# Rows of an attention layer's residual: turned by TensorE before, by 32x32 blocks on VectorE and by DMA after

## The chip, the core and the metric

One core of a Trainium2 chip runs the whole program. TensorE (PE) multiplies matrices, VectorE (DVE), ScalarE (ACT) and GpSimd (POOL) do the elementwise work, SyncE (SP) and, for small things, ACT and POOL issue DMAs. The metric is device time of one execution in microseconds; before the change it is 2252.64 us, the median of 3 runs (2251.83 to 2252.95). All data are float32.

## What is computed

The input x is 16 batches of 1024 nodes with 256 features, with one adjacency matrix for all. Each batch goes through two residual layers; the first holds a small network with two attentions (one over all nodes, one masked), the second one masked attention. Cut to what matters:

```python
# layer 0
h = maximum(layernorm(x), 0)
out = relu(h @ mlp1_w + b1); residual = out                # 256 -> 512
out = elu(gat(out, None, W_fc, a_fc, slope=0.2))           # over all 1024 nodes
out = relu((elu(out) + residual) @ mlp2_w + b2)            # 512 -> 256, "o" below
res2 = out
out = elu(gat(out, adj, W_hand, a_hand, slope=0.2)) + res2 # masked
x = x + relu(out)
# layer 1
h = maximum(layernorm(x), 0)
x = x + relu(masked_softmax_attention(h @ W, a, adj, slope=0.01))
# gat(v): g = v @ W; e[i,j] = leaky_relu(f1[i] + f2[j]); softmax over j; sum_j att[i,j] g[j]; elu
```

The order of the nodes is free wherever it is summed over (index j), as long as the mask's rows and the vectors of a sum follow the same order.

## The kernel before

**Tiling.** 1024 nodes are 8 tiles of 128, in two halves of 4 tiles (`NH` = 2, `TH` = 4). A matrix product contracts over the partitions, so layers that contract over features need features on the partitions ("turned", names that end in T), while the attention's sum and the residual of a batch need nodes on the partitions ("natural"). Turning is done in two ways. `Norm.turn` (L529) and `Dense.natural` (L1030) use transposes of 128x128 on TensorE into PSUM, from which ACT copies them out. `BlockNorm` (L553, first norm of batches 3 to 15) uses VectorE's transpose, which turns each 32x32 block in its place (L572), and then 16 DMAs a half from SP (L582, `move`), which put the blocks where they belong; in those each contiguous run has 32 floats, 128 bytes.

**Stages of a batch.** First norm, `mlp1` (L748), projection for the dense attention (`h`, L762), dense attention through sorting: ranks on DVE (L808 to L815), a scatter of rows by POOL into DRAM (L822), a read of the sorted rows (L866), running sums on DVE (L896, L909) written as tables (L901), gathers from these by POOL (L934: eight "fine", then eight "coarse" that add onto them), the mean (L956, L959), `merge` (L1006 to L1017) back into `resT`. Then `mlp2` (L1024) gives `oT`, two chunks of features by 1024 nodes. `oT` is used twice: as the stationary operand of the projection `pa` (L614) of the first masked attention, and, turned to natural rows, as its residual `o_nat`. `natural` makes `o_nat` for batch b in 4 steps of 4 transposes and one eviction (L1038, L1040), which also subtracts 1. The masked attention makes weights on DVE (L667, `att`, a ring of 8 buffers of 128x256), multiplies (L677) and finishes: two rectified copies (L692, L693), two exponentials (L698, L699), two adds on POOL (L705 with `o_nat`, L706), and DVE's `update` (L710) into x. Second norm, its projection `pb`, a second masked attention (`ob`), and the store.

**Order.** The batches overlap. Nothing is scheduled by the compiler: each step has a nominal time, given by `at` (L471) relative to the batch's base (one base every 142 units), plus a shift from the table `SHIFT` for its place in the list; the steps are sorted by time, and each engine's instructions, those of PE, DVE, ACT and SP, stand in that order. POOL's are held in the same order by dependencies. So an engine that waits for one instruction holds back all behind it. The table has parts: "start", "first" (batch 0), "mid" (1 to 12), "end" (13 to 15). For the mid batches, times relative to the batch's own base:

- `masked_first8`: the 4 steps of `natural` at 4.5, 26.0, 18.2 and 30.2;
- `second_mlp2`: the projections of `oT`, -16.7 to -8.5;
- `masked_first6`: x loaded again at 10; `start51`: the xn of a later batch loaded at 38.7;
- `first_norm7`, `first_norm8`: the moves of the first norm, in the period before;
- `masked_first4`/`masked_first3`: the row of weights, written to DRAM by ACT (`send`) and read back on all partitions by SP (L652).

What a move issues, and the way `o_nat` is made:

```python
for q in range(P // Q):                                     # L580
    nc.sync.dma_start(dst[q * Q:(q + 1) * Q, :, a, :],
                      src[a * Q:(a + 1) * Q, :, q, :])
...
nc.tensor.transpose(ps[:, u * F + c * P:u * F + (c + 1) * P],   # L1038
                    self.oT[:, c, t * P:(t + 1) * P], ident)
...
nc.scalar.activation(self.o_nat[:, 2 * q:2 * q + 2, :],         # L1040
                     ps.rearrange("p (u f) -> p u f", u=2), AF.Identity, bias=neg1)
```

## Time and profile before

| What | Value |
|---|---|
| Median of 3 runs | 2252.64 us |
| Profiled execution, own time | 2251.37 us |
| Its span, first to last instruction | 2249.6 us |
| Granted TensorE clock, mean | 0.998 |
| One steady period (base to base) | 134.2 us |
| DVE, ACT, POOL busy in it | 99 to 101, 77 to 78, 60 to 62 us |
| DMA share and rate in it | 0.65, 169 to 175 GB/s |
| DMA packets in all | 263,870; 124,352 under 512 B |
| Moves of the first norm (hT<-xn) | 416 DMAs of 32 KB |
| First adds of `o_nat` in POOL (L705) | x118, 904 ns |

A line of a group reads: line, engine, operation, output<-inputs, shapes, count, then busy time and mean of one, then the idle time of the engine just before such instructions, and what ended it. In a timeline a line is a run of like instructions: start, length, engine, line, what, count, and in brackets the idle time before it with the one that ended it. In a table of stages the columns are the stage, its length, the busy time of PE, PEld (weight loads), DVE, ACT and POOL with their counts, the granted clock, the share of the DMA engines and GB/s. A busy PE is counted to the modelled end of each matmul; consecutive matmuls overlap.

### The profile page before, as it was taken

How to read it: one execution, taken by the hardware profiler on the slowest of the kernel's cores; microseconds unless marked ns; L12 is line 12 of the kernel's file. 1: busy time of each engine (PE TensorE's matmuls, PEld its weight loads, DVE VectorE, ACT ScalarE, POOL GpSimd, SP SyncE). 2: the span in 40 equal slices, each digit the busy share in tenths (PEclk: the TensorE clock that was granted, in tenths of full speed). 3: DMA queues.
4: the chain of work that ended last, by engine and by line, in shares of the span. 5: the costliest groups of instructions: out<-in, count | busy, mean ns of one | idle time of the engine just before them, and what ended most of it. 6: DMA issues, size and time to landing. Idle time of an engine off the chain costs nothing.

```text
span 2249.6 us, 31025 instructions
## 1 busy us (share of the span) xinstructions
PE 2207.2 (98%) x9754; PEld 1723.4 (77%) x9754; DVE 1643.1 (73%) x4535; ACT 1259.6 (56%) x2797; POOL 954.4 (42%) x1212
## 2 busy tenths in 40 slices
PE   7999999999999999999999999999999999999997
PEld 5767777787877878787787877878787787877776
DVE  7677676777867678776776867677786776858765
ACT  5355745547365564756557375564746557365542
POOL 1163425263452536425263452636435263543620
PEclk9999999999999999999999999999999999999999
DMA  5568466675766757566685666757566585645700
GB/s 197 159 175 196 114 208 154 186 183 148 197 123 200 187 168 190 137 196 148 192 191 147 189 127 194 188 177 189 130 205 144 185 197 153 164 125 169 178 22 28
DMA packets 263870, 368.95 MB, mean 164 GB/s; under 512 B 124352, under 2 KB 175880, under 8 KB 259600
## 3 DMA queue, kind: packets, MB, share of 16 engines
q1 hardware_dynamic: 217088, 202.72, 31.9%
q0 software_dynamic: 45952, 163.99, 28.9%
q8 instruction: 80, 1.31, 0.3%
q14 instruction: 94, 0.77, 0.1%
q10 hardware_dynamic: 656, 0.17, 0.0%
HBM read 226.88 MB, written 126.29 MB: 157 GB/s over the span
## 4 chain that ended last, share of the span: by engine, by line
PE 75%; DVE 6%; DMA 2%; POOL 2%; ACT 1%; issue 1%; POOLq 0%; DVEq 0%; ACTq 0%; SPq 0%
PE oa L677 17%; PE h L762 16%; PE ob L677 14%; PE m L1024 8%; PE m L748 6%; PE pa L614 4%; PE pb L614 3%; PE hpT L1006 2%; DMA got<-coarse,k 2%; DVE attb L667 1%; PE carry L918 1%; PE on L1038 1%; PE nt L536 1%; DVE stats L516 1%; DVE hp L959 1%
## 5 line engine op out<-in xcount | busy, mean ns | idle before, releaser
L677 PE MATMUL ob<-hmb,attb 128*128 128x257 f32 x2048 | 463.9, 380 | 2.2 <-DVE attb L667 1.9
L762 PE MATMUL h<-wfc_sb,resT 128*128 128x257 f32 x2048 | 462.8, 379 | 0.0
L677 PE MATMUL oa<-hma,atta 128*128 128x258 f32 x2048 | 459.9, 382 | 1.8 <-DVE atta L667 1.5
L677 PEld LDWEIGHTS ob<-hmb,attb 128*128 128x128 f32 x2048 | 383.9, 190 | 67.2 <-issue 12.3
L677 PEld LDWEIGHTS oa<-hma,atta 128*128 128x128 f32 x2048 | 384.8, 190 | 59.3 <-DVE atta L667 2.9
L762 PEld LDWEIGHTS h<-wfc_sb,resT 128*128 128x128 f32 x2048 | 380.1, 189 | 59.1 <-issue 7.4
L705 POOL TENSOR_TENSOR posa<-posa,onat 128x256 f32<-128x256 f32 x118 | 106.7, 904 | 546.1 <-ACT posa L693 487.6
L667 DVE SCALAR_TENSOR_TENSOR attb<-rowsb,qwdb,edge 128x256 f32<-128x256 f32 (+1 forms) x536 | 292.1, 563 | 34.6 <-PE ob L677 28.6
L667 DVE SCALAR_TENSOR_TENSOR atta<-rowsa,qwda,edge 128x256 f32<-128x256 f32 (+1 forms) x520 | 257.3, 524 | 51.4 <-DMA rowsa<-row_a 35.6
L934 POOL DMA_INDIRECT got<-coarse,k x124 | 203.4, 1640 | 90.9 <-DMA got<-fine,k 56.6
L748 PE MATMUL m<-hT,w_sb 128*128 128x512 f32 x512 | 236.6, 596 | 1.9 <-ACT rb L719 1.1
L1024 PE MATMUL m<-resT,w_sb 128*128 128x512 f32 x512 | 228.3, 593 | 1.0 <-POOL resT L1017 1.0
L719 ACT ACTIVATE rb<-ob,recb 128x256 f32<-128x256 f32 x128 | 58.5, 474 | 274.9 <-DVE recb L717 248.9
L1017 POOL TENSOR_TENSOR resT<-resT,e 128x512 f32<-128x512 f32 x128 | 165.5, 1295 | 104.9 <-DVE e L1016 96.7
L692 ACT ACTIVATE ea<-oa,reca 128x256 f32<-128x256 f32 x128 | 60.3, 471 | 248.1 <-DVE reca L689 228.7
L934 POOL DMA_INDIRECT got<-fine,k x124 | 126.7, 1022 | 128.5 <-DVE hpd L999 41.9
L1024 PEld LDWEIGHTS m<-resT,w_sb 128*128 128x128 f32 x512 | 94.5, 190 | 102.4 <-issue 93.5
L748 PEld LDWEIGHTS m<-hT,w_sb 128*128 128x128 f32 x512 | 94.2, 191 | 89.0 <-issue 74.7
L822 POOL DMA_INDIRECT sorted<-hnat,place x128 | 128.6, 1004 | 53.9 <-DVE place L815 33.0
L764 ACT COPY hnat<-h 128x257 f32<-128x257 f32 x256 | 90.8, 367 | 104.1 <-PE h L762 101.6
L845 ACT ACTIVATE junk<-r,fs 128x1024 int8<-128x1024 f32 x124 | 142.6, 1150 | 0.9 <-POOL fs L766 0.6
L1016 DVE SCALAR_TENSOR_TENSOR e<-hpT,e 128x512 f32<-128x512 f32 x128 | 87.9, 688 | 53.2 <-ACT e L1010 53.0
(195 smaller groups left out, 3391.2 us busy)
## 6 DMA issues: line engine op xcount, KB each, us to landing
xs<-sorted SPq DMA_DIRECT2D x32, 1028.0 KB
fine<-tt SPq DMA_DIRECT2D x32, 1026.0 KB
fine<-xs SPq DMA_DIRECT2D x32, 1026.0 KB
x<-in_x_dram SPq DMA_DIRECT2D x16, 1024.0 KB
xn<-in_x_dram SPq DMA_DIRECT2D x15, 1024.0 KB
out_dram<-x SPq DMA_DIRECT2D x28, 512.0 KB
hT<-xn SPq DMA_DIRECT2D x416, 32.0 KB
coarse<-carry SPq DMA_DIRECT2D x32, 256.5 KB
```

The source lines that it names most:

```text
L614: nc.tensor.matmul(ps[:, :2 + F], lhsT=hT[:, c, t * P:(t + 1) * P], rhs=self.w_sb[:, c, 0, :], start=(c == 0), stop=(c == FC - 1))
L667: nc.vector.scalar_tensor_tensor(a_t[:, :n * P], self.rows[:, i], self.qwd[:, 1, j:j + 1], edge[:, j, i], op0=OP.max, op1=OP.mult)
L677: nc.tensor.matmul(self.out[t][:, :F + self.ONES], lhsT=self.att[t0, j][:, (t - t0) * P:(t - t0 + 1) * P], rhs=self.hm[:, j, 2:2 + F + sel ...
L705: adder.tensor_add(pos, pos, o_nat[:, t, :])
L748: nc.tensor.matmul(ps, lhsT=w1_sb[:, kc, c * P:(c + 1) * P], rhs=piece(kc, h), start=(kc == 0), stop=(kc == FC - 1))
L762: nc.tensor.matmul(ps[:, :F + 1], lhsT=self.resT[:, kc, t * P:(t + 1) * P], rhs=wfc_sb[:, kc, g, :], start=(kc == 0), stop=(kc == HC - 1))
L764: nc.scalar.copy(self.h_nat[:, t, g, :], ps[:, :F + 1])
L822: made = nc.gpsimd.indirect_dma_start(out=sorted_d[self.b % 2], out_offset=bass.IndirectOffsetOnAxis(ap=self.place[:, t:t + 1], axis=0), i ...
L845: nc.scalar.activation(junk, self.r2, AF.Sign, bias=self.fs[:, 0, t:t + 1], accum_out=self.signs[:, t:t + 1])
L934: nc.gpsimd.indirect_dma_start(out=got[u // n][:, u % n, :], out_offset=None, in_=(coarse_d if coarse else fine_d)[self.b % 2][:, :], in_o ...
L1017: nc.gpsimd.tensor_add(dst, dst, e)
L1024: nc.tensor.matmul(ps, lhsT=w2_sb[:, kc, c * P:(c + 1) * P], rhs=self.resT[:, kc, h * HALF:(h + 1) * HALF], start=(kc == 0), stop=(kc == H ...
```

## The change

`o_nat` of batches 1 to 13 is no longer made by TensorE. DVE turns `oT` in place by 32x32 blocks, a half at a time (`Dense.blocks`), and eight `move` steps of four DMAs each bring the blocks to the partitions of their nodes. So that the DMAs have runs of 1 KB, the features and nodes of a half are laid out anew (`by_rows`): a turned half is a row of four parts of 256 floats, part a holding the nodes whose place in their tile is 32a to 32a+31, from all four tiles. A tile of a turned tensor (`sources`) is then not 128 consecutive nodes but one such part: nodes are permuted within a half wherever they are summed over. `mlp2`, both norms and `mlp1` write and read through that view; the mask's columns are permuted when it is built, and the rows of weights are put back in natural order on their way (`send_row`, `row`). The first norm's moves take the same form, with runs of 1 KB in place of 128 bytes. Batches 0, 14 and 15 still turn on TensorE; since a tile of theirs is now not contiguous, ACT copies each 128x128 piece first. The subtraction of 1 goes from `natural` into the two `update`s. Nearly all entries of `SHIFT` are new (cut below to the ones that the text speaks of).

```diff
-    "mid masked_first8": (0, 19.91, 10.5, 20.85,),
+    "mid masked_first8a": (-7.062,),
+    "mid masked_first8b": (0, 12.185, 12.037, 0, -3.284, 0, 12.142, 11.934,),
-    "mid second_mlp2": (-9.69, -9.64, -7.39, -8.59, -7.35, -8.45, -11.04, -8.66,),
+    "mid second_mlp2": (-13.877, -13.654, -13.893, -15.403, -15.718, -17.262, -17.592, -18.455,),
-    "mid start51": (4.72,),
+    "mid start51": (-41.029,),
...
-        nc.vector.tensor_scalar(valid, valid, wrong[:, 1, t:t + 1], None, op0=OP.max)
+        by_tile = work.tile([P, N], BF16, tag="hp", name=f"by_tile_{t}", bufs=TH)
+        for h in range(NH):
+            lo = h * HALF
+            nc.vector.tensor_scalar(
+                by_tile[:, lo:lo + HALF].rearrange("p (a u i) -> p u a i", u=TH, i=Q),
+                valid[:, lo:lo + HALF].rearrange("p (u a i) -> p u a i", u=TH, i=Q),
+                wrong[:, 1, t:t + 1], None, op0=OP.max)
...
-            nc.tensor.transpose(pt[:, j, :], valid[:, j * P:(j + 1) * P], ident16)
+            nc.tensor.transpose(pt[:, j, :], by_tile[:, j * P:(j + 1) * P], ident16)
...
-    def send_row(dst, col, name):
+    def send_row(dst, col, name, by_tile=False):
...
-        nc.scalar.dma_start(dst.rearrange("o (u i) -> (o u) i", i=P), line)
+        if by_tile:
+            for h in range(NH):
+                nc.scalar.dma_start(
+                    dst[:, h * HALF:(h + 1) * HALF].rearrange("o (u a i) -> (o a) u i", u=TH, i=Q),
+                    line[half(h)].rearrange("a (u i) -> a u i", u=TH))
+        else:
+            nc.scalar.dma_start(dst.rearrange("o (u i) -> (o u) i", i=P), line)
     class Norm:
...
         def turn(self, t):
...
-                self.hT = big.tile([P, FC, N], F32, tag=self.tag, name=f"hT{self.name}", bufs=1)
+                self.hT = big.tile([P, NH, FC * HALF], F32, tag=self.tag, name=f"hT{self.name}",
+                                   bufs=1)
...
-                    nc.scalar.activation(self.hT[:, c, h * HALF:(h + 1) * HALF], self.ps[c],
+                    nc.scalar.activation(by_rows(self.hT[:, h])[:, c],
+                                         self.ps[c].rearrange("p (u a i) -> p u a i", u=TH, i=Q),
...
         def piece(self, c, h):
-            return self.hT[:, c, h * HALF:(h + 1) * HALF]
+            return by_rows(self.hT[:, h])[:, c]
+        def part(self, c, t):
+            return sources(self.hT, c, t)
         def stats_steps(self, h):
...
+        def turned(self, h):
+            return self.get_x()[:, half(h)].rearrange("p t f -> p (t f)")
         def blocks(self, t):
...
-            dst = self.get_x()[:, half(h)].rearrange("p t f -> p (t f)")
-            dst = dst.rearrange("p (c u n) -> p c u n", c=FC, u=TH)
-            nc.vector.transpose(dst[:, :, u, :], self.hn[t])
+            dst = self.turned(h).rearrange("p (q c u i) -> p u c q i", q=P // Q, c=FC, u=TH)
+            nc.vector.transpose(dst[:, u], self.hn[t].rearrange("p (c q i) -> p c q i", c=FC, i=Q))
         def move(self, h, a):
...
-                self.hT = big.tile([P, NH, FC * HALF], F32, tag="hT0", name=f"hT{self.name}",
+                self.hT = big.tile([P, NH, FC * HALF], F32, tag=self.tag, name=f"hT{self.name}",
...
-            src = self.get_x()[:, half(h)].rearrange("p t f -> p (t f)")
-            src = src.rearrange("p (v q i) -> p v q i", q=P // Q, i=Q)
-            dst = self.hT[:, h].rearrange("p (v a i) -> p v a i", a=P // Q, i=Q)
-            for q in range(P // Q):
-                nc.sync.dma_start(dst[q * Q:(q + 1) * Q, :, a, :],
-                                  src[a * Q:(a + 1) * Q, :, q, :])
-        def piece(self, c, h):
-            return self.hT[:, h, c * HALF:(c + 1) * HALF]
+            move_blocks(self.hT[:, h], self.turned(h), a)
+    def move_blocks(dst, src, a):
+        run = FC * HALF // (P // Q)
+        for q in range(P // Q):
+            nc.sync.dma_start(dst[q * Q:(q + 1) * Q, a * run:(a + 1) * run],
+                              src[a * Q:(a + 1) * Q, q * run:(q + 1) * run])
+    def sources(wide, c, t):
+        h, a = divmod(t, TH)
+        lo = (a * FC + c) * P
+        return wide[:, h, lo:lo + P]
+    def by_rows(t):
+        return t.rearrange("p (a c u i) -> p c u a i", a=P // Q, c=FC, i=Q)
     def half(h):
...
-        def __init__(self, get_hT, w_sb, slope, b, which):
-            self.get_hT, self.w_sb, self.slope, self.name = get_hT, w_sb, slope, f"{which}_{b}"
+        def __init__(self, get_part, w_sb, slope, b, which):
+            self.get_part, self.w_sb, self.slope, self.name = get_part, w_sb, slope, f"{which}_{b}"
...
-            hT = self.get_hT()
+            part = self.get_part()
...
-                nc.tensor.matmul(ps[:, :2 + F], lhsT=hT[:, c, t * P:(t + 1) * P],
+                nc.tensor.matmul(ps[:, :2 + F], lhsT=part(c, t),
...
         def send(self):
-            send_row(row_d[self.which][self.b % 2], self.qwd[:, 0, :], f"line{self.name}")
+            send_row(row_d[self.which][self.b % 2], self.qwd[:, 0, :], f"line{self.name}", True)
         def row(self, sent=False):
...
-                for i in (slice(0, PAIR), slice(PAIR, N)):
-                    nc.scalar.copy(self.rows[:, i], rows_ps[:, i])
+                for h in range(NH):
+                    i = slice(h * HALF, (h + 1) * HALF)
+                    nc.scalar.copy(self.rows[:, i].rearrange("p (u a i) -> p a u i", u=TH, i=Q),
+                                   rows_ps[:, i].rearrange("p (a u i) -> p a u i", u=TH, i=Q))
...
         def add(self, t, o_nat, adder):
...
-            adder.tensor_add(pos, pos, o_nat[:, t, :])
+            wide = pos.rearrange("p (c a i) -> p c a i", c=FC, i=Q)
+            adder.tensor_add(wide, wide, o_nat(t))
...
         def update(self, t, xt):
-            nc.vector.scalar_tensor_tensor(xt[:, t, :], self.out[t], 0.0, xt[:, t, :], op0=OP.max,
+            nc.vector.scalar_tensor_tensor(xt[:, t, :], self.out[t], 1.0, xt[:, t, :], op0=OP.max,
...
     class Gnn1(Masked):
...
         def update(self, t, xt):
-            nc.vector.tensor_add(xt[:, t, :], xt[:, t, :], self.out[t])
+            nc.vector.scalar_tensor_tensor(xt[:, t, :], xt[:, t, :], -1.0, self.out[t], op0=OP.add,
+                                           op1=OP.add)
...
         def mlp2(self, h, c):
...
-                self.oT = big.tile([P, FC, N], F32, tag="hT", name=f"oT_{self.b}", bufs=1)
+                self.oT = big.tile([P, NH, FC * HALF], F32, tag="hT", name=f"oT_{self.b}", bufs=1)
...
-            nc.scalar.activation(self.oT[:, c, h * HALF:(h + 1) * HALF], ps, AF.Relu,
+            nc.scalar.activation(by_rows(self.oT[:, h])[:, c],
+                                 ps.rearrange("p (u a i) -> p u a i", u=TH, i=Q), AF.Relu,
...
+        def part(self, c, t):
+            return sources(self.oT, c, t)
+        def blocks(self, h):
+            nc.vector.transpose(self.oT[:, h], self.oT[:, h])
+        def move(self, h, a):
+            if self.o_nat is None:
+                self.o_nat = big.tile([P, NH, FC * HALF], F32, tag="onat", name=f"onat_{self.b}",
+                                      bufs=1)
+            move_blocks(self.o_nat[:, h], self.oT[:, h], a)
+        def natural_rows(self, t):
+            return (self.o_nat[:, t // TH].rearrange("p (a c u i) -> p u c a i", a=P // Q, c=FC,
+                                                     i=Q)[:, t % TH])
         def natural(self, q):
...
-                self.o_nat = big.tile([P, NT, F], F32, tag="onat", name=f"onat_{self.b}", bufs=1)
+                self.o_nat = big.tile([P, NH, FC * HALF], F32, tag="onat", name=f"onat_{self.b}",
+                                      bufs=1)
...
+            h, u0 = divmod(2 * q, TH)
...
-                    t = 2 * q + u
-                    nc.tensor.transpose(ps[:, u * F + c * P:u * F + (c + 1) * P],
-                                        self.oT[:, c, t * P:(t + 1) * P], ident)
-            nc.scalar.activation(self.o_nat[:, 2 * q:2 * q + 2, :],
-                                 ps.rearrange("p (u f) -> p u f", u=2), AF.Identity, bias=neg1)
+                    nodes = by_rows(self.oT[:, h])[:, c, u0 + u]
+                    line = work.tile([P, P], F32, tag="part", name=f"line_{self.b}_{q}_{u}_{c}")
+                    nc.scalar.copy(line.rearrange("p (a i) -> p a i", i=Q), nodes)
+                    nc.tensor.transpose(ps[:, u * F + c * P:u * F + (c + 1) * P], line, ident)
+            for u in range(2):
+                nc.scalar.copy(self.natural_rows(2 * q + u),
+                               ps[:, u * F:(u + 1) * F].rearrange("p (c a i) -> p c a i", c=FC,
+                                                                  i=Q))
...
-        gnn0[b] = Gnn0(lambda b=b: dense[b].oT, wh_sb, SLOPE_A, b, "a")
-        gnn1[b] = Gnn1(lambda b=b: norm2[b].hT, wl_sb, SLOPE_B, b, "b")
+        gnn0[b] = Gnn0(lambda b=b: dense[b].part, wh_sb, SLOPE_A, b, "a")
+        gnn1[b] = Gnn1(lambda b=b: norm2[b].part, wl_sb, SLOPE_B, b, "b")
...
-            at("masked_first8", t0 + 4.5, t0 + 11, each(dense[b].natural, range(NT // 2)))
+            if b == 0:
+                at("masked_first8", t0 + 4.5, t0 + 11, each(dense[b].natural, range(NT // 2)))
+            else:
+                d = dense[b]
+                at("masked_first8a", t0 + 0.5, t0 + 2, each(d.blocks, range(NH)))
+                at("masked_first8b", t0 + 3, t0 + 13, each(d.move, range(NH), range(P // Q)))
...
-            at("masked_first11", end + 1.2, end + 1.2, [lambda t=t: m.combine(t, dense[b].o_nat)])
+            at("masked_first11", end + 1.2, end + 1.2, [lambda t=t: m.combine(t, dense[b].natural_rows)])
...
-                at("masked_first12", end + 2.6, end + 2.6, [lambda t=t: m.add(t, dense[b].o_nat, nc.vector)])
+                at("masked_first12", end + 2.6, end + 2.6, [lambda t=t: m.add(t, dense[b].natural_rows, nc.vector)])
```

## The prediction, made before the result was seen

> **What bounds the kernel now.** I read the busy times first, then the groups by line with shapes kept apart, then one steady period in order of time, then the same period cut into stages.
>
> ```profile
> PE 2207.2 (98%) x9754; PEld 1723.4 (77%) x9754; DVE 1643.1 (73%) x4535; ACT 1259.6 (56%) x2797; POOL 954.4 (42%) x1212
> ...
> L748 PE MATMUL m<-hT,w_sb 128*128 128x512 f32 x512 | 236.6, 596 | 1.9 <-ACT rb L719 1.1 <-ACT hT L540 0.6 <-issue 0.2
> ...
> L1038 PE MATMUL on<-ident,oT 128*128 128x128 f32 x256 | 38.0, 273 | 0.1
> ```
>
> TensorE works in 2207.2 of 2249.6 us. Of the 42.4 us without it, 11.1 lie before its first matmul (it waits for POOL's rstd) and about 10 behind its last product; half of the rest lies in the last batches (93% busy from 2100 to 2200 us). In the steady periods, 134.2 us each, it is busy for all 134.2. So the price of an edit in the middle is what it adds to or takes from TensorE, as long as nothing makes it wait. The busy column is not that price: matmuls overlap, and 273 ns is one latency. The pace stands in the timeline of TensorE, where a row merges a run:
>
> ```profile
> 1110.69 0.60 PE L1038 MATMUL on<-ident,oT 128*128 128x128 f32 x4
> 1111.13 7.13 PE L677 MATMUL oa<-hma,atta 128*128 128x258 f32 x32
> 1118.09 0.60 PE L1038 MATMUL on<-ident,oT 128*128 128x128 f32 x4
> 1118.53 4.52 PE L677 MATMUL oa<-hma,atta 128*128 128x258 f32 x20
> 1122.88 0.60 PE L1038 MATMUL on<-ident,oT 128*128 128x128 f32 x4
> 1123.32 11.56 PE L677 MATMUL oa<-hma,atta 128*128 128x258 f32 x52
> ```
>
> From the start of four transposes to the next product are 0.44 us: 109 ns each. Whether entering such a group costs more is open: runs of products take 0.2177 us each here ((7.13 - 0.38)/31, 0.38 being one latency), by which 32 end just where the next transposes begin; elsewhere they take 0.2143 (14.73 us for 68), by which 0.1 us would be lost: 0 to 0.07 us a group.
>
> **What goes.** Batches 1 to 13 lose `natural`: 13 x 16 = 208 transposes on TensorE and 13 x 4 = 52 evictions on ACT. TensorE: 208 x 0.109 = 22.7 us, and 52 entries at 0 to 0.07, 0 to 3.6; I take 1.3, together **-24 us** (1.8 per period). ACT: 52 x 0.68 = 35 us, not on the path. [...] the rows say 109 ns, as they run back to back, and that TensorE has no free time while DVE has 27%. I go by the rows.
>
> **What is added for it.** Per batch two DVE block transposes of 128x1024 and eight moves of four DMAs (32 KB each). The nearest DVE row:
>
> ```profile
> L572 DVE STREAM_TRANSPOSE xn<-hn 128x256 f32<-128x256 f32 x104 | 42.4, 427 | 0.0
> ```
>
> An estimate from it and the DVE slope between 256 and 512 elements (429 and 688 ns, L710 and L1016, 1.01 ns each): 0.43 + 768 x 0.00101 = 1.2 us, 2.4 us a period. They stand at base -6.6 and +1.2 (nominal times of the table; `on` at base +4.5 ran at 1097.27 us here, that at 18.2 at 1110.69). They wait for the projections that read oT; those stand at base -20, so nothing is held behind them. DVE has gaps there:
>
> ```profile
> 1093.89 0.17 DVE L621 TENSOR_REDUCE exta<-hma 128x1 f32<-128x8 f32 x1 [4.67 <-ACT hma L616]
> ...
> 1105.95 1.28 DVE L667 SCALAR_TENSOR_TENSOR atta<-rowsa,qwda,edge 128x256 f32<-128x256 f32 x3 [4.22 <-DMA rowsa<-row_a]
> ```
>
> Two idle stretches of over 4 us, before the first weights of the masked products: 0 on the end. If that cover is gone, 2.4 us a period of DVE in a stage that has none to spare (below).
>
> The moves on SP: the old ones are the measure.
>
> ```profile
> 1119.11 10.98 SPq L901 DMA_DIRECT2D fine<-xs  x2
> 1130.14 0.50 SPq L335 DMA_DIRECT2D xn<-in_x_dram  x1
> ...
> 1201.31 10.43 SPq L582 DMA_DIRECT2D hT<-xn  x16
> ```
>
> Sixteen issues in 10.43 us, 0.65 each, so 32 new ones take 21 us of SP per period. Half 0's are due at base +3, 16.4, 17.5 and 6.75, half 1's at 4.7, 9.25, 22.6 and 23.7. The first passes ahead of the row's read, while SP idles for it (1092.8 to 1101.3). Two of half 0 queue behind the first table write (issued 1102.2 now), and done by some 1110; two of half 1 queue behind the write of 1119.1, done by some 1127 (8 x 0.65 plus the flight). The first adds that read `o_nat` ran at 1119.05 (tile 0) and about 1134 (tile 4). Margin 7 us or more: 0 on the end. Behind a late move stand the other table writes on SP, and POOL's add, and behind that the gathers.
>
> The first norm's moves become 1-KB runs (416 x 256 packets of 128 B become 416 x 32 of 1 KB). Nothing waits for hT in the steady part (L748's idle is 1.9 us in the run), so 0.
>
> **Layout edits.** mlp1's moving operand becomes 16 runs of 32 floats instead of 512 in a row. No row has such an operand. Below: 0; above: some tenth of its pace (0.43 us, from 1.88 = 3 paces + 0.59), 512 x 0.043 = 22 us. [...] No run here shows it; I take 0. Strided outputs of ACT and DVE: L572's write is already in 32-float runs at 427 ns against 424 for a plain add (L723), so 0. POOL's adds read `o_nat` in 32-float runs: 0 to +0.39 us each (up to the 1295 ns of the 512-wide add, from 904), at most 3.1 us a period on an engine 42% busy; 0, with up to 1.6 us for the four adds between gathers if it bites. The second DMA of `send` costs ACT 0.27 us, 27 times, ahead of time: 0. Masks: 8 DVE writes of 486 ns become 16 shorter strided ones, 0 to 4 us at 20-50 us; I take 1. update's new forms: 429 against 424 ns, 0.
>
> **Batches 0, 14 and 15** keep `natural`, with an ACT copy before each transpose, from a ring of two buffers. A copy is about 0.31 us (414 ns at 256 elements, L698, less 128 x 0.83 ns, slope to L1009's 626). Copies 3 and 4 need transposes 1 and 2 to be over; so TensorE, in order, waits inside each step: 0.27 (transpose) + 0.31 + 0.14 (weight load) - 0.22 + another 0.2 = 0.7 to 0.8 us. Behind the waiting copy stand, on ACT, the scales of hm and the evictions of products, for which TensorE's next banks wait. Twelve steps: **+9 us**; the lower end 0, where TensorE waits anyway (last batch), the upper 20, if ACT's queue is late. I take +7.
>
> **New places.** Two matter. The load of the next xn moves from base +38.7 to base -7.0, in front of the sorted read on SP; the stages show what it leaves:
>
> ```profile
> 1110.00:1120.00 10.00, 10.00 (x51) 8.75 (x51) 10.00 (x25) 3.26 (x8) 0.95 (x1) 1.00 0.47 140
> ...
> 1130.00:1140.00 10.00, 10.00 (x48) 8.74 (x47) 9.83 (x31) 4.00 (x11) 5.34 (x7) 1.00 1.02 220
> ...
> 1160.00:1170.00 10.00, 10.00 (x51) 8.59 (x50) 2.02 (x8) 4.46 (x12) 8.69 (x10) 1.00 1.01 188
> ```
>
> Columns: TensorE, weight loads, DVE, ACT, POOL busy, granted clock (1.00), DMA share, GB/s. DMA is full from 1130 on, when the xn load starts; 1 MB at 220 GB/s is 4.8 us that the gathers get back. It matters, because the gathers end without margin:
>
> ```profile
> 1169.99 0.16 DVE L946 TENSOR_TENSOR den<-got,qd 128x4 f32<-128x4 f32 x1 [6.81 <-DMA got<-coarse,k]
> ...
> 1174.69 0.36 PEld L1006 LDWEIGHTS hpT<-ident,hp 128*128 128x128 f32 x3 [0.29 <-DVE hp L959]
> ```
>
> DVE stands 6.81 us for the gathered rows, and TensorE takes up hp just as it comes. With 1.8 us less TensorE work ahead of it, it would stand here unless the gathers come earlier: 4.8 against 1.8 says that they do. The second: the projections of oT go from base -17...-8 to -20, so the row for the masked weights comes earlier and DVE's 4.22 us shrink, just ahead of the stage where DVE is full (10.00 of 10). I count neither as a gain beyond that, and 0 for the rest of the table.
>
> **Sum.** -24 + 7 + 1 = -16 us. Span 2249.6 becomes 2233.6; this execution took 2251.37, 1.8 more than its span, and the median shown is 1.3 above that. So 2252.6 - 16 = about **2236 us**.
>
> **Rivals.**
> - *The gathers set the period (slower).* Place: hpT at L1006. For: no margin above; xn's load now competes with the sorted read that feeds the same chain. Against: its window was under 80% full. If the chain is as long as before, all 24 us are given back as waits, and the 8 of batches 0, 14, 15 and the masks remain: 2261. It decides from about 1.2 us of new wait per period (16/13). Chance 0.14.
> - *DVE full at 1110-1140.* TensorE reaches the masked products 1.3 us earlier than DVE has weights; for: 10.00 of 10; against: eight weight buffers are 8 x 0.86 = 6.9 us ahead, and the row comes earlier. Half the gain lost: 2252.6 - 12 + 8 = 2249. Chance 0.12.
> - *mlp1's operand is slower.* At the upper bound, +22: 2259; breaks even at 31 ns a matmul (16/512). Chance 0.04.
> - *More falls away*: no waits in batches 0, 14, 15 and 7 us of the scattered ones gone: 2252.6 - 24 + 1 - 7 = 2223. Chance 0.12.
> - The forecast, 2227 to 2245: 0.58.
>
> Measurements of this kernel tell about 0.2% (4.5 us) from no change. Faster: 0.58 + 0.12 + half of DVE's case, 0.76; within: 0.08; slower: 0.16. The range 2219 to 2253 leaves out the two slow cases.
>
> **What would show it.** A steady period of about 132.4 us with TensorE busy throughout; `on` left x48; hpT's wait on hp no longer than now; L946's wait shorter; TensorE idle inside `natural` of batches 0, 14, 15; L748's mean still 596 ns. Wrong, if the period stays at 134 with waits on hp or atta, if POOL waits for the moves of o_nat, or if L748 grows.

## The result, and the profile after

The changed kernel takes 2294.74 us (median of 4 runs, 2288.7 to 2299.17), the kernel before beside it 2252.8 (2251.83 to 2255.87): ratio 1.0183, with 95% interval 1.0171 to 1.0195. The forecast was 2236, range up to 2253; the kernel became 42 us slower. Profiled execution: 2293.65 us, span 2291.9.

The page of the kernel after, its busy times and two groups of its lines (busy us, mean ns | idle before, releasers):

```profile
PE 2213.4 (97%) x9546; PEld 1698.8 (74%) x9546; DVE 1639.5 (72%) x4569; ACT 1253.0 (55%) x2805; POOL 972.4 (42%) x1212
...
L800 PE MATMUL m<-hT,w_sb 128*128 128x512 f32 x512 | 237.9, 599 | 1.5 <-ACT resT L803 1.0 <-ACT hT L576 0.5
...
L1111 PE MATMUL on<-ident,line 128*128 128x128 f32 x48 | 11.9, 318 | 7.2 <-ACT line L1110 4.0 <-DVE qwda L691 3.0
```

The 208 transposes are gone (9754 matmuls became 9546), and mlp1's strided operand costs next to nothing (599 ns for 596). The engine that works most beyond before is POOL, 18 us on an engine 42% busy. So the 42 us are not longer work but waits, and what waits bring with them (last section). To count them I take, for each matmul, the time from its start to the next one's start, less the pace of its size (0.109, 0.217 or 0.429 us for 128, 256 or 512 columns in runs of like matmuls in these traces). Over the whole trace this excess was 35.4 us before and is 104.7 now: 69.3 more, against 22.7 us of transposes saved. The rest, 46.6 us, is what the stretch from the first matmul to the last grew by; what lies ahead of and behind it became 4.3 us shorter, so the span grew by 42.3. Most of it is in the twelve steady periods (third start of `extpsa` to the fifteenth): 7.0 us before, 71.8 now. Where it sits, in TensorE's waits of the kernel after (tile, line, releaser: us in total, times, longest):

```profile
PE oa L727 <- DVE atta L717: 16.9, 29, 1.6
PE extpsb L520 <- DVE extb L670: 15.3, 9, 2.8
PE linea_ps L525 <- ACT qwda L687: 11.6, 13, 0.9
...
PE on L1111 <- ACT line L1110: 4.0, 13, 0.7
```

The same two in the kernel before, where `linea_ps` had no wait:

```profile
PE oa L677 <- DVE atta L667: 1.5, 3, 0.7
PE extpsb L491 <- DVE extb L622: 0.8, 1, 0.8
PE extpsb L491 <- DVE extb L621: 0.8, 1, 0.8
```

A steady period (start of `extpsa` to the next, mean of ten) went from 134.5 to 138.3 us; 132.4 was forecast. TensorE's timeline in one such period, with the idle time and its releaser in brackets:

```profile
1112.83 0.29 PE L520 MATMUL extpsa<-ident,exta 128*128 128x128 f32 x1
1114.01 0.27 PE L525 MATMUL linea_ps<-ident,qwda 128*8 128x128 f32 x1 [0.89 <-ACT qwda L687]
...
1118.42 4.50 PE L727 MATMUL ob<-hmb,attb 128*128 128x257 f32 x20
1123.84 1.98 PE L727 MATMUL oa<-hma,atta 128*128 128x258 f32 x8 [0.92 <-DVE atta L717]
...
1195.70 0.29 PE L520 MATMUL extpsb<-ident,extb 128*128 128x128 f32 x1 [1.16 <-DVE extb L670]
```

`linea_ps` stands directly behind `extpsa`, with no other matmul to cover the short chain between them on DVE and ACT. Before, four matmuls of `mlp1` stood there:

```profile
1095.33 0.27 PE L491 MATMUL extpsa<-ident,exta 128*128 128x128 f32 x1
1095.44 1.88 PE L748 MATMUL m<-hT,w_sb 128*128 128x512 f32 x4
1097.16 0.27 PE L496 MATMUL linea_ps<-ident,qwda 128*8 128x128 f32 x1
```

For the other two waits, DVE's timeline in the same period:

```profile
1123.20 3.65 DVE L717 SCALAR_TENSOR_TENSOR atta<-rowsa,qwda,edge 128x256 f32<-128x256 f32 x9 [5.76 <-DMA rowsa<-row_a]
...
1194.06 1.42 DVE L1011 SCALAR_TENSOR_TENSOR hp<-got,den,part 128x513 f32<-128x513 f32 x2
1195.40 0.16 DVE L669 TENSOR_REDUCE extb<-hmb 128x1 f32<-128x8 f32 x1
```

DVE stood idle 5.76 us for the row, 4.22 before (all 13 such waits: 67.3 us, 35.6 before); TensorE then waits for the weights. And `extb` stands behind two `hp`, 1.42 us together; before, it stood ahead of them:

```profile
1170.68 0.16 DVE L621 TENSOR_REDUCE extb<-hmb 128x1 f32<-128x8 f32 x1
...
1171.64 2.96 DVE L959 SCALAR_TENSOR_TENSOR hp<-got,den,part 128x513 f32<-128x513 f32 x4 [0.72 <-ACT part L956]
```

### The profile page after: what moved, and what is told of

It reads as the page before. It is cut to its first block, busy times and chain, and to the rows that moved or that the text cites. A ratio compares the mean times of both kernels' runs of the same rounds, so it can differ in the third digit from the quotient of the medians.

```text
span 2291.9 us, 31196 instructions
## 1 busy us (share of the span) xinstructions
PE 2213.4 (97%) x9546; PEld 1698.8 (74%) x9546; DVE 1639.5 (72%) x4569; ACT 1253.0 (55%) x2805; POOL 972.4 (42%) x1212
## 5 line engine op out<-in xcount | busy, mean ns | idle before, releaser
L727 PE MATMUL oa<-hma,atta 128*128 128x258 f32 x2048 | 465.6, 383 | 19.5 <-DVE atta L717 16.9
L727 PE MATMUL ob<-hmb,attb 128*128 128x257 f32 x2048 | 472.6, 381 | 1.4 <-DVE attb L717 1.2
L756 POOL TENSOR_TENSOR posa<-posa,onat 128x256 f32<-128x256 f32 x118 | 113.6, 963 | 470.6 <-ACT posa L743 205.6
L717 DVE SCALAR_TENSOR_TENSOR atta<-rowsa,qwda,edge 128x256 f32<-128x256 f32 (+1 forms) x520 | 255.2, 527 | 79.2 <-DMA rowsa<-row_a 67.3
L717 DVE SCALAR_TENSOR_TENSOR attb<-rowsb,qwdb,edge 128x256 f32<-128x256 f32 (+1 forms) x536 | 251.5, 504 | 8.8 <-PE ob L727 6.8
L986 POOL DMA_INDIRECT got<-fine,k x124 | 134.1, 1081 | 77.7 <-DVE stats L551 40.8
L1060 DVE TENSOR_SCALAR e<-hpT 128x512 f32<-128x512 f32 x128 | 86.6, 688 | 70.9 <-PE hpT L1058 68.0
```

Of the source, the lines that this page charges most:

```text
L717: nc.vector.scalar_tensor_tensor(a_t[:, :n * P], self.rows[:, i], self.qwd[:, 1, j:j + 1], edge[:, j, i], op0=OP.max, op1=OP.mult)
L727: nc.tensor.matmul(self.out[t][:, :F + self.ONES], lhsT=self.att[t0, j][:, (t - t0) * P:(t - t0 + 1) * P], rhs=self.hm[:, j, 2:2 + F + sel ...
L756: adder.tensor_add(wide, wide, o_nat(t))
L986: nc.gpsimd.indirect_dma_start(out=got[u // n][:, u % n, :], out_offset=None, in_=(coarse_d if coarse else fine_d)[self.b % 2][:, :], in_o ...
L1060: nc.vector.tensor_scalar_min(e, ps, 0.0)
```

## The experiments

All 18 in one table; "before" is the kernel before, timed beside each of them, the period as above.

| run | median us | before | ratio (95%) | period |
|---|---|---|---|---|
| changed kernel | 2294.74 | 2252.8 | 1.0183 (1.0171 to 1.0195) | 138.3 |
| e1 new code, old places | 2393.85 | 2250.04 | 1.0639 (1.0618 to 1.0660) | 141.3 |
| e2 old code, new places | 2285.43 | 2250.04 | 1.0153 (1.0136 to 1.0169) | 138.9 |
| e3 old places, moves later | 2352.51 | 2252.4 | 1.0438 (1.0419 to 1.0457) | 140.6 |
| e4 changed, extb earlier | 2289.25 | 2252.4 | 1.0170 (1.0152 to 1.0187) | 137.4 |
| e5 changed, filler earlier | 2292.18 | 2252.4 | 1.0175 (1.0158 to 1.0192) | 138.2 |
| e6 e3, load of x earlier | 2335.72 | 2250.71 | 1.0361 (1.0335 to 1.0388) | 138.6 |
| e7 e3 without moves | 2265.13 | 2250.71 | 1.0056 (1.0039 to 1.0073) | 133.9 |
| e8 changed, without moves | 2289.96 | 2250.71 | 1.0172 (1.0155 to 1.0189) | 137.5 |
| e9 e6, moves in gaps | 2334.16 | 2251.55 | 1.0361 (1.0336 to 1.0387) | 139.6 |
| e10 e9 without moves | 2260.57 | 2251.55 | 1.0034 (1.0020 to 1.0049) | 134.5 |
| e11 e6, last table on time | 2362.69 | 2251.82 | 1.0488 (1.0455 to 1.0521) | 142.4 |
| e12 before, table write behind xn | 2251.72 | 2251.82 | 0.9998 (0.9989 to 1.0007) | 134.3 |
| e13 changed, sums earlier | 2314.64 | 2251.82 | 1.0272 (1.0252 to 1.0292) | 139.8 |
| e14 e11, sums earlier | 2361.61 | 2251.82 | 1.0480 (1.0462 to 1.0497) | 142.4 |
| e15 changed, gathers first | 2313.31 | 2252.65 | 1.0268 (1.0234 to 1.0303) | 140.6 |
| e16 before, adds first | 2293.32 | 2252.65 | 1.0184 (1.0166 to 1.0201) | 137.9 |
| e17 e15 and filler | 2316.73 | 2252.65 | 1.0291 (1.0271 to 1.0310) | 140.0 |
| e18 before, first norm new | 2252.44 | 2251.96 | 1.0003 (0.9995 to 1.0012) | 134.4 |

### Code and places apart (e1, e2)

e1 is the changed code with the table of offsets (SHIFT) of the kernel before, e2 the code before with the table of the changed kernel. In e1 one block transpose of the first norm stands ahead of the centring of another tile, so that tile is normed from overwritten rows; the work is the same. Two entries of the table in e1, changed kernel to e1 (e2 goes the other way):

```diff
-    "mid masked_first6": (-23.765,),
-    "mid masked_first11": (-4.467, -5.066, -4.218, -4.817, -1.377, -1.981, -7.997, -8.596,),
+    "mid masked_first11": (-2.15, -5.21, 0, 0, 0, -2.21, 4.2,),
```

> The changed kernel's code with the table SHIFT of before (the new steps, which that table doesn't name, stand at their nominal times). The kernel before takes 2253 us, the changed one 2295. Theory P (the moved steps cost it: TensorE lost its filling work around the row of weights and got extb late): the steady period falls to about 132.5, the waits oa<-atta (16.9 us), extpsb<-extb (15.3) and linea_ps<-qwda (11.6) of the changed kernel are gone, and the time is 2225 to 2240 us. Theory C (the code costs it: two DMAs for a row, the moves ahead of the row's read on SP, strided adds): the waits stay, with a period of about 138 and 2285 to 2300 us. In between, if both have a share.

> The code of before with the changed kernel's table SHIFT. Theory P: the same waits at extpsb, linea_ps and oa as in the changed kernel, on top of the transposes that are still there: a period of 139 to 140, 2305 to 2325 us. Theory C: the places are harmless, 134 a period and 2248 to 2260 us.

The new places alone cost 35 us. TensorE's waits in e2, columns as before:

```profile
PE extpsb L478 <- DVE extb L609: 18.8, 10, 2.5
PE linea_ps L483 <- ACT qwda L626: 11.6, 13, 0.9
...
PE oa L664 <- DVE atta L654: 3.9, 12, 1.1
```

The first two are those of the changed kernel, `linea_ps` to the number: they come with the places, not with the turn of the rows. The excess of the whole trace rose from 35.4 to 77.1 us, as much as the span of this trace (41.6 us); it is the slowest of e2's four runs. The new table has no offset for the transposes of `natural` in batches 1 to 12, so in e2 these stand at their nominal times, ahead of the masked products and no longer between them. That belongs to the 35 us too. The new code in the old places costs 144 us; most of it in waits for `atta` (4.36 us a period) and in batches 0, 14 and 15, where the transposes of `natural` waited 44 us.

### The moves in the old order, and no moves (e3, e6, e7, e8, e9, e10)

e3 takes e1's worst away: the copies that `natural` needs are issued as a step of their own, two for four transposes, three units earlier; the block transposes and moves get offsets that put them behind the row's read. e6 loads x earlier, e9 spreads the moves into gaps of SP (it also puts DVE's first update three units later and the copies of batches 14 and 15 earlier). e7, e8 and e10 are e3, the changed kernel and e9 without moves: the adds of batches 1 to 13 read the rows of batch 0.

```diff
 e3
+    'mid masked_first8a': (-7.062,),
+    'mid masked_first8b': (10.1, 8.95, 7.8, 6.65, 10.1, 8.95, 14.6, 13.45),
...
+                nc.scalar.copy(line[:, c].rearrange("p u (a i) -> p u a i", i=Q),
+                               by_rows(self.oT[:, h])[:, c, u0:u0 + 2])
 e6, on e3
+    'mid masked_first6': (-16.2,),
 e9, on e6
-    'mid masked_first8b': (10.1, 8.95, 7.8, 6.65, 10.1, 8.95, 14.6, 13.45),
+    'mid masked_first8b': (2.8, 1.65, 7.6, 6.45, 17.1, 15.95, 14.8, 13.65),
 e7, e8, e10: move
-            move_blocks(self.o_nat[:, h], self.oT[:, h], a)
+            self.o_nat = dense[0].o_nat
```

> The changed kernel's code with the table of before again, but the new steps not at their nominal times: the eight moves of o_nat stand on SP behind the row's read (half 0 behind the first table write, half 1 before and behind the third), the two block transposes as in the changed kernel, and in batches 0, 14 and 15 the copies ahead of the transposes are one step of its own, 3 units earlier, two copies for four transposes. Theory P (moved steps, and in the last run the new steps standing ahead of the row's read): TensorE has 22.7 us less work and its waits are about those of before plus the 0.44 us a period of filling transposes that are missing; 2230 to 2240 us. Theory C (two row DMAs, POOL's strided adds, DVE's 2.5 us a period of block transposes): waits on atta and on POOL's chain stay, 2255 us or more.

> The run before in the old order (moves behind the row's read, 2352 us) with one step moved: x is loaded 16 units earlier in the steady periods, so that this 1-MB load no longer stands between the row's read and the moves of o_nat. In that run 16 moves took 17.45 us to issue, not 10.4, and POOL's first add waited for them. Theory Q (the moves are late because they share the queue with 1-MB transfers, and POOL's adds, DVE's updates and the weights behind them wait in turn): 2235 to 2265 us. If only part of it is the load and the 1-MB table write in front of the moves is as bad, 2290 to 2330.

> The same kernel in the old order (x loaded where it was) with the 32 DMAs per batch that move o_nat left out; batches 1 to 13 add the residual rows of batch 0 instead of their own. DVE's block transposes, the two row DMAs and the strided adds stay. Theory Q: all of its loss is the moves, so 2228 to 2240 us, about 13 to 24 under the kernel before. If the strided adds, the blocks or the two row DMAs cost, 2250 us or more.

> The changed kernel in its own order with the same 32 DMAs per batch left out (batches 1 to 13 add the rows of batch 0). Theory P (in that order it is the moved steps that cost, not the moves): 2280 to 2296 us, as with them. If the moves cost there too (the row's read behind them, the queue, POOL's waits), 2225 to 2260.

> The new code in the old order, with the moves in the gaps of SP: of half 0 two moves before the row's read (SP idles there) and two behind the first table write, half 1 wholly between the third and the fourth table write, so that no table write stands behind moves; x loaded early; DVE's update of tile 0 three units later, so that the weights behind it don't wait for POOL's first add; the copies of batches 14 and 15 earlier. The run without moves in the old order took 2265 us, the one with late moves and early x 2336. Theory Q (moves cost by what stands behind them on SP and by DVE waiting for the add that needs them): most of the 70 us between these two go, 2250 to 2275 us. If the moves' own DMA traffic is the cost, it stays above 2300.

> The same kernel with the moves left out (batches 1 to 13 add the rows of batch 0). What is then left above 2253 - 22.7 = 2230 us is the price of the rest: missing filling work, DVE's block transposes, batches 0, 14 and 15. With DVE's update later and the copies earlier, 2240 to 2258 us; if these two edits do nothing, 2265.

Moves in the old order cost 71 to 87 us (e7 to e6 and to e3), 74 in gaps (e10 to e9); in the new order about 5 (e8 to the changed kernel), less than their intervals tell apart. So the new order made room for the moves, and its price is the 35 us of e2. What the moves do in the old one, in the timeline of SP's issues in e3, then POOL's and TensorE's in the same stretch:

```profile
1142.85 0.38 SPq L310 DMA_DIRECT2D x<-in_x_dram  x1
1143.83 0.37 SPq L906 DMA_DIRECT2D fine<-tt  x1
1144.25 17.45 SPq L577 DMA_DIRECT2D onat<-oT  x16
```

```profile
1163.14 0.72 POOL L708 TENSOR_TENSOR posa<-posa,onat 128x256 f32<-128x256 f32 x1 [30.83 <-DMA onat<-oT]
```

```profile
1168.51 11.52 PE L679 MATMUL oa<-hma,atta 128*128 128x258 f32 x44 [2.80 <-DVE atta L669]
```

Behind the load of x (1 MB) and a table write, sixteen issues take 17.45 us, 1.09 each, where the measure of the prediction was 0.65. POOL's first add starts when the move lands. Its 30.83 us of idle time are not the price of that: before the change POOL stood idle 28.98 us at this place, for ACT. The price is the lateness: in the steady periods the add starts 24.0 us behind `linea_ps` in e3 and 21.0 without moves (e7). DVE's update of x waits 4.60 us for it, and TensorE 2.80 us for the weights that stand behind the update on DVE. The last table write, also behind moves on SP, is issued 39.1 us behind `linea_ps`, 31.9 in e7. Loading x earlier (e6) mends 17 us of the loss; the rest stayed in every old order tried.

Without moves the gain of the transposes should show. It doesn't. e8 has 22.7 us less TensorE work than e2 and ends where e2 does (2283.41 to 2291.6 against 2285.24 to 2293.23). In the traces the waits for `atta` are 13.5 us longer in e8, and `on` loses 12.2 in batches 0, 14 and 15. (These are e8's fastest run and e2's slowest, so the shorter period of e8 in the table is no proof of a gain.) e7 in the old order is 14 us slower than before: of 1.7 us a period (16 transposes) 0.6 stay (134.5 to 133.9; `oa` waits 0.86 a period more than its pace), and `on` gives 15.0 back. e10, with the copies early and DVE's update late, has `on` down to 3.9 us, but a period of 134.5 as before: `oa` waits 1.70 us in each, 0.07 before, and that is nearly all that the transposes were. Its waits for `atta` in the whole run (1.5 us before), then two stages of one period:

```profile
PE oa L680 <- DVE atta L670: 12.7, 25, 2.7
```

```profile
1115.00:1120.00 5.00, 4.91 (x24) 3.94 (x23) 5.00 (x13) 0.84 (x2) 0.00 (x0) 1.00 0.36 136
1120.00:1125.00 5.00, 4.62 (x22) 3.72 (x21) 5.00 (x12) 2.35 (x7) 1.28 (x2) 1.00 0.43 115
```

DVE has no free time there (5.00 of 5), so TensorE, with no transposes between its products, waits for DVE instead.

### Mending the new waits one by one (e4, e5)

```diff
 e4, on the changed kernel
-    "mid second_norm1": (1.448, 2.556, 10.768, 10.3, 0, 0.251, 0, -1.484,),
-    "mid second_norm2": (6.347,),
+    "mid second_norm1": (1.448, 2.556, 4.02, 3.24, 0, 0.251, 0, -1.484,),
+    "mid second_norm2": (4.35,),
 e5, on the changed kernel
-    "mid first_mlp1": (0, 12.333, 0, 15.759,),
+    "mid first_mlp1": (0, 0, 0, 15.759,),
```

> The changed kernel with one place mended in the steady periods: two projections of the second masked attention ahead of a filling mlp1 step, and DVE's extb reductions ahead of the gathered rows' den and hp instead of behind them. Theory P: the 17 us of extpsb's wait go and stay gone, 2276 to 2284 us. If the gathers or DVE bound the period anyway, the wait comes back at hpT or oa and the time stays at 2290 to 2296.

> The changed kernel with one step moved in the steady periods: the third of the four mlp1 products (1.7 us of TensorE) stands ahead of the masked products of the first attention instead of inside them, so that TensorE has 10.5 us of work between extpsa and the first masked product where the row takes 11. If only the missing filling work costs, the waits oa<-atta fall by about 1.1 us a period: 2278 to 2284 us. If DVE, which has the weights and the running sums to make after the row has come, is the bound of that stage, the wait only moves further back in the run of masked products: 2290 to 2298 us.

Neither can be told from the changed kernel. TensorE's waits in e4, then in e5:

```profile
PE hpT L1022 <- DVE hp L975: 7.2, 23, 1.2
```

```profile
PE extpsb L484 <- DVE extb L634: 23.9, 10, 2.7
```

In e4 the wait for `extb` is gone, and `hpT`'s wait for `hp` has come in its place; in e5 the excess of `oa` fell from 31.3 to 27.0 us and that of `extpsb` rose from 17.1 to 25.9. So neither wait by itself sets the period: taken away at one place, much of it comes up at another.

### What sets the new period (e11 to e17)

Two theories. Either the last table write sets it (its issue lies 36.5 us behind `linea_ps` in the changed kernel, 32.0 before), or POOL's first gather (52.5 against 41.8): the new places put the last two adds of `combine` ahead of the gathers.

```diff
 e11, on e6
-    'mid masked_first8b': (10.1, 8.95, 7.8, 6.65, 10.1, 8.95, 14.6, 13.45),
+    'mid masked_first8b': (10.1, 8.95, 7.8, 6.65, 10.1, 8.95, 7.8, 6.65),
 e12, on the kernel before
-    "mid dense_sums9": (2.53,),
+    "mid dense_sums9": (6.8,),
 e13, on the changed kernel
-    "mid dense_sums6": (11.143,),
+    "mid dense_sums6": (5.0,),
+    "mid dense_sums9": (-4.6,),
 e14, on e11
-    'mid dense_sums9': (2.53,),
+    'mid dense_sums9': (-0.7,),
 e15, on the changed kernel
-    "mid masked_first11": (-4.467, -5.066, -4.218, -4.817, -1.377, -1.981, -7.997, -8.596,),
+    "mid masked_first11": (-4.467, -5.066, -4.218, -4.817, -1.377, -1.981, 1.603, 2.004,),
 e16, on the kernel before
-    "mid early_gathers1": (0, 9.89,),
-    "mid masked_first11": (-2.15, -5.21, 0, 0, 0, -2.21, 4.2,),
+    "mid early_gathers1": (4.8, 9.89,),
+    "mid early_gathers2": (3.9, 3.9,),
+    "mid masked_first11": (-2.15, -5.21, 0, 0, 0, -2.21, -1.3, -2.1,),
 e17 is e15 with the edit of e5
```

(e13 and e14 also move the running sums, `dense_sums7`, up to 4.75 and 3.2 units earlier; e11 also the copies of batches 14 and 15.)

> Theory L, formed from the traces so far: the steady period is a loop, from the row of the first masked weights over DVE's running sums to the write of the last table for the gathers, then gathers, mean, merge, mlp2, projection and the next row. In the eleven traces the last table's write stands 31.8 to 38.9 us behind linea, and the period is that plus 101 to 103 (plus 105.5 in one); TensorE's waits only show where it is long. This run is the kernel with early x load and moves behind the row (2336 us, last table written at 36.5, behind moves) with the four moves of half 1 all ahead of the third table write, so that the last table doesn't stand behind any. L: last write at about 33, period 134.5, 2255 to 2270 us. If the moves cost by their traffic or by POOL's adds, it stays at 2315 or more.

> The kernel before with one step moved in the steady periods: the write of the last table stands on SP behind the 1-MB load of the next xn instead of ahead of it. No engine's instructions are touched and nothing is added. L: the table lands about 4 to 5 us later, and so the period is 3 to 5 us longer: 2285 to 2315 us. If TensorE's work alone bounds the kernel before, with margin in the gathers: 2250 to 2258 us.

> The changed kernel with DVE's last running sums and the two last table writes earlier in its steady periods (the sums up to 4.8 units, ahead of some of the weights). L: the last table is written at 33 to 34 us behind linea instead of 36.5, the period falls by 2 to 3 us, and so do the waits extpsb, linea_ps and hp: 2258 to 2272 us, although no wait of TensorE was mended at its place and the weights come later. If the waits come from the places at which they show, 2290 or more.

> The first kernel of this call with the last four running sums 1 to 3 units and the last table write 3 units earlier. L: last write at about 30, so that the loop is 132 and TensorE's work (132.3 a period) is the bound again: 2240 to 2255 us. If the weights that stand behind the sums cost as much as the table gains: 2260 or more.

> The theory of the last table (L) is out: with that table late the kernel before stayed at 2252, with it early the changed kernel went up. What remains constant over all traces is the time from POOL's first gather to the next linea: 91.5 to 92.6 us in the old order, 85.2 to 86.3 in the new one. Theory G: the first gather sets the period, and in the new order it comes late (52.5 us behind linea, 41.8 before) because POOL must first do all eight adds of o_nat, the last two of which need the end of the masked products; in the old order three gathers stand ahead of the last two adds. This run is the changed kernel with those two adds of the steady periods behind three gathers. G: first gather at about 46, the waits at extpsb and hpT go, a period of 135 to 136: 2255 to 2272 us. If the gathers have slack, 2288 to 2298.

> The reverse in the kernel before: the adds of tiles 6 and 7 ahead of the first three gathers, nothing else. G: first gather at 46 to 49 us instead of 41.8, the period 3 to 6 us longer, with new waits at hpT or extpsb: 2285 to 2325 us. If the gathers have slack, 2250 to 2260.

> The first kernel of this call with the third mlp1 product ahead of the masked products as well, which alone gave 2.5 us. If G is right and the gathers no longer bind, the filling work is now worth what it covers, 1 to 1.7 us a period: 2235 to 2258 us. Else 2285 or more.

No run decides between them in the changed kernel. The table write first: e13 brought its issue from 36.5 to 33.4 us behind `linea_ps`, and the period grew; but the last weights went from 40.5 to 41.9 with it. e11 (34.4 for e6's 36.9) and e14 were slower than e6. e12 missed its aim: the write waits for its data on SP and was issued 32.1 us behind `linea_ps` as before; the edit only let the load of xn go ahead of it, which costs nothing. Now the gathers. In the kernel before, the two adds ahead of them cost 41 us (e16), as much as the whole change. POOL's timeline in e16, then TensorE's:

```profile
1165.43 0.72 POOL L677 TENSOR_TENSOR posa<-posa,onat 128x256 f32<-128x256 f32 x1 [6.17 <-ACT posa L665]
...
1174.09 1.04 POOL L494 TENSOR_TENSOR rstd<-rstd,power 128x4 f32<-128x4 f32 x1
```

```profile
1176.89 0.79 PE L508 MATMUL nt<-ident,hn 128*128 128x128 f32 x4 [0.81 <-DVE hn L498]
```

The add waits 6.17 us for ACT, and everything behind it on POOL with it: `rstd` starts 54.9 us after `linea_ps` (1119.18), 51.1 before, and TensorE waits for the rows normed with it. The changed kernel doesn't lose its time by this path: there `rstd` stands ahead of the last adds, 40.8 us behind `linea_ps` (1114.01):

```profile
1154.83 1.05 POOL L557 TENSOR_TENSOR rstd<-rstd,power 128x4 f32<-128x4 f32 x1
```

In the changed kernel the opposite edit (e15, e17) makes it slower, not faster: `m` now waits 2.81 us a period, for ACT's `rb`. But it also missed its aim. The first gather came at 50.1 us behind `linea_ps` for 52.5, where about 46 was expected, because it then waited for the last table:

```profile
1177.73 1.16 POOL L950 DMA_INDIRECT got<-fine,k  x1 [2.29 <-DMA fine<-xs]
```

These waits are 35.8 us in e15, up to 5.4 each, with the table written at 36.4. So the two theories hang together: with the adds moved away, the table holds the gathers. e13 had only the table earlier, e15 only the adds moved; no run did both in the changed kernel. And what stands behind the gathers isn't fixed either: from the first gather to the next `linea_ps` it was about 86 us, which the expectation of e15 took as constant, and became 90.5. So one moved pair of steps can cost as much as the change lost; that it is this pair there is not shown. Which dependence sets the changed kernel's period stays open.

### The first norm alone (e18)

The kernel before with only the first norm's new layout, its moves in 1-KB runs, and mlp1's strided operand:

```diff
-                nc.sync.dma_start(dst[q * Q:(q + 1) * Q, :, a, :],
-                                  src[a * Q:(a + 1) * Q, :, q, :])
+                nc.sync.dma_start(self.hT[q * Q:(q + 1) * Q, h, a * run:(a + 1) * run],
+                                  src[a * Q:(a + 1) * Q, q * run:(q + 1) * run])
...
-            return self.hT[:, h, c * HALF:(c + 1) * HALF]
+            wide = self.hT[:, h].rearrange("p (a c u i) -> p c u a i", a=P // Q, c=FC, i=Q)
+            return wide[:, c]
```

> One part of the change alone in the kernel before: the first norm of batches 3 to 15 in the new layout (its moves with runs of 1 KB, mlp1 reading runs of 32 floats), o_nat still turned by TensorE, the old order (one block transpose 1.2 units later, since it now overwrites rows of all four tiles). If the layout is free and nothing waits for it, as the prediction has it: 2248 to 2256 us, with the pace of mlp1 still 0.43 us. If the fewer packets leave room for the gathers and loads: 2240 to 2247. If the strided operand or the wider write costs: 2260 or more.

No difference, as the prediction said for this part. From the page of e18:

```profile
DMA packets 170686, 368.95 MB, mean 164 GB/s; under 512 B 17856, under 2 KB 82696, under 8 KB 166416
```

263870 packets became 170686, those under 512 B 17856 from 124352, and the time stayed: nothing waited for them.

## Why the prediction was wrong, step by step

- **"New places. Two matter … and 0 for the rest of the table."** This step failed. Of the two it looked at, the load of xn seems to do what it said: DVE's waits for the gathered rows fell from 100.1 to 18.4 us, and TensorE's for `hp` from 2.0 to none. But the rows don't come earlier: the gathers start later (above), and DVE takes up the first rows 78.9 us behind `linea_ps`, 73.2 before. For the projections see the next point. The rest, priced at 0, cost 35 us (e2), more than twice the whole gain forecast (16 us). I read the few moves with a large offset and took the others to be neutral, though the prediction's own first finding was that TensorE has no slack in a period: then every changed pair of neighbours on an engine is a possible wait. Two could be read from the order of the steps beforehand: `linea_ps` directly behind `extpsa` (11.6 us), and `extb` behind `hp` (15 to 19). With the waits for `atta` they are where the loss shows; what sets the period behind them stays open (e4, e5, e11 to e17).
- **"so the row for the masked weights comes earlier and DVE's 4.22 us shrink"**: wrong in sign. The first weights came 9.1 us behind `linea_ps` for 7.3, and DVE idled 67.3 us for 35.6.
- **"What goes … together −24 us"**: the work went (a period's work at the paces fell from 134.0 to 132.3 us), the time did not. This is the second step that failed: of 1.7 us a period e10 keeps nothing and e7 0.6, and the medians of e8 and e2 show nothing. The transposes were also filler between products, in a stage in which DVE is full (5.00 of 5 us in e10). The rival "DVE full at 1110-1140" named this place and gave half the gain back; in e10 all of it went.
- **"Batches 0, 14 and 15 … I take +7"**: 11.9 us, inside the bounds (0 to 20). In old places without early copies it was 44, in e9 and e10 with early ones 3.9.
- **"Margin 7 us or more: 0 on the end"**, the moves: in the new order within 5 us of right; in the old order, whose times the prediction used for the margin, they cost 71 to 87. There the term that failed is the price of an issue (1.09 us each in e3, not 0.65) and with it the margin.
- **mlp1's operand, 1-KB runs, block transposes**: right, though no trace of before showed the 0 for the operand. 599 and 597 ns (596 before); e18 the same time; 1240 ns for a 128x1024 block transpose against an estimate of 1.2 us. The masks' +1 and the second DMA of `send` were not tried by themselves.
- The rival *gathers set the period* had the sign and named a wait of `hpT` for `hp`. In the changed kernel this wait is absent; it appears when `extb` is mended (e4). That the gathers are the cause is not shown, so the sign was no proof of the rival.

No version tried beats the kernel before; the nearest are e12 and e18, which are the same.

## What to carry to other kernels

In a schedule written out by hand with an engine at 98%, price the reordering as its own change: list each instruction's new neighbour on its engine and ask what now stands between a result and its use. Work taken from the busiest engine gains only where the operands of what follows come earlier too; if it stood in front of a wait, it was the cover of that wait (in e10, 1.70 us of waits a period in place of 1.7 us of transposes). Before blaming the wait that a profile shows, move it away: if the time stays, the cause lies elsewhere.

## What the runs showed of the hardware that was not expected

A wait of TensorE cost twice in places. The stretch of e3 whose 2.80 us wait was shown, cut into stages (length, TensorE, weight loads, DVE, ACT, POOL busy, granted clock, DMA share, GB/s):

```profile
1168.00:1170.00 2.00, 1.49 (x4) 1.22 (x5) 2.00 (x8) 1.35 (x4) 0.00 (x0) 0.73 0.08 21
1170.00:1172.00 2.00, 2.00 (x6) 1.59 (x5) 2.00 (x4) 1.94 (x5) 1.45 (x2) 0.50 0.78 289
1172.00:1174.00 2.00, 2.00 (x9) 1.69 (x9) 1.98 (x3) 0.02 (x1) 1.92 (x3) 0.92 1.09 247
```

After the wait the granted clock is below 1 in all three stages and 0.50 in the middle one, and the 44 products take 11.37 us to the next start (1168.51 to 1179.88), where 44 paces of 0.217 are 9.55: 1.8 us more. The trace of the changed kernel has five stretches at a clock of 0.50 between 60 us and the last 60, four of 3.41 us and one of 6.83. In the first, from 505.00 us, the products of 257 columns start every 0.43 us in place of 0.22, the transposes every 0.21 in place of 0.11. Three of the five stand behind gaps of 2.65 to 3.37 us between two starts, the other two, in batches 14 and 15, behind several gaps of 1.0 to 1.8 us close together. Four more gaps of 2.64 to 3.03 us have none behind them, and neither has the single 1.2 us of `linea_ps`. So which wait brings a stretch is not shown. Counted between 60 us and the last 60: none before, 20 us of half clock in the changed kernel, 14 in e2, 75 in e3, 82 in e11 (mean granted clock of these whole traces: 0.998, 0.995, 0.995, 0.983, 0.981). As the products start half as often, half of it is about the most that they cost, by this estimate: 10 of the 42 us here, 7 of e2's 35, 41 of e11's 111. So part of a large loss can be this second cost; no run takes it away by itself.
